# Summing experts' results by accumulating DMA in a graph and mixture-of-experts kernel

## The chip, the cores and the metric

The kernel runs on one core of a Trainium2 chip. The metric is the device time of one execution in microseconds (us), the median of several runs. The engines are named as in the profile: PE is TensorE (matrix products), PEld its weight loads, DVE is VectorE, ACT is ScalarE, POOL is GpSimd, SP is SyncE. SP, ACT and POOL issue DMAs; indirect DMAs (gathers and scatters by a list of rows) are issued by POOL.

## The reference

3125 nodes with 256 features each pass through four layers, each added to the nodes' rows: a graph convolution of three layers, a mixture of experts, a graph attention, and a second mixture of experts. The change is in the two mixtures. The first one has 16 experts:

```
gate_logits = x @ gate_w + gate_b
topk_vals, topk_idx = jax.lax.top_k(gate_logits, K)          # K = 2
topk_w = jax.nn.softmax(topk_vals, axis=-1)
h = jax.nn.relu(jnp.einsum('bsh,ehf->bsef', x, w1) + b1)
expert_out = jnp.einsum('bsef,efh->bseh', h, w2) + b2
sel = jnp.take_along_axis(expert_out, topk_idx[:, :, :, None], axis=2)
moe = jnp.sum(topk_w[..., None] * sel, axis=2)
y = x + moe                                                   # then a layer norm over y
```

The second has 8 experts, weights that are the softmax over all of them, GELU for ReLU, and adds the weighted sum to the nodes' rows without a norm; that is the kernel's output. In both, a node's result is its base row plus two experts' rows, each times a weight. The second bias b2 of an expert is part of its row.

## The kernel before

A tile is 128 nodes on 128 partitions; there are 25 node tiles (`NT`) of which 125 rows each are real. The expert stages don't work by node tile but by token tile: 128 tokens of one expert. A `Router` does this for each mixture.

`steps` computes the gate for some node tiles, chooses two experts a node, and scatters for each choice a record of eight numbers into `slots`, a list in HBM that is ordered by expert. `metas` holds the records: 0 is the place of the result, 1 the second expert, 2 and 3 the weights, 5 the node's number. `keep` writes the normalised rows into `feats` in HBM, from which they are gathered later. `steps` also fills `cw`, a table of nodes by experts with the weights. `plan` counts the tiles of each expert; `mine` has a 1 where token tile j belongs to expert e. `clear`, early in the kernel, fills the unused records and the unused result rows.

`experts` runs over token tiles: 58 in the first mixture, 54 in the second. For tile j, `fetch` loads its records (`slot`, L1021, by SP or ACT) and gathers its rows (`xs`, L1023, by POOL); `turned` transposes them (L1032, PE; L1034, DVE); `first` multiplies with w1, whose 512 KB SP loads per tile (L1009, L1044), and ACT applies the function (L1048); `second` multiplies with w2 into `py` (L1054). DVE then computes where the row goes and its weight g (L1061 to L1068), multiplies `py` by g into `y` (L1070), and POOL scatters y to rows of `res` in HBM (L1071). `res` has two rows a node, one per choice, and a row for each unused place, so every scattered row has a place of its own and the kernel declares the scatters independent of each other. The function `behind` keeps PE's and SP's instructions of this loop in the written order: products of tile j+1 with w1, transposes of tile j+2, products of tile j with w2. POOL's queue is filled by the scheduler, in which gathers run nine tiles ahead of the scatters.

The bias b2 is added by node tile, not by token tile: `cw` of a node tile is transposed and multiplied with b2 and added to the node's base row in SBUF. Eight node tiles are done before the loop (L1094 to L1107), the other 17 beside token tiles 8 to 24 (`bias`, L1081 to L1086).

After the loop, `results` loads the two result rows of each node (L1153, 256 KB a node tile), and PE adds them to the base row by three products with the identity (L1156), which ACT copies to SBUF (L1157). In the first mixture the layer norm, the transposes and products for the attention follow block by block (L1524 to L1549). In the second, each node tile goes to the output by two DMAs, from ACT and SP (L1745), 112 and 13 rows.

Of the kernel before, what the change touches and what calls it, by code (L numbers as in the profile page):

```python
# [19 lines left out]
P = 128  # L20
# [574 lines left out]
def fast(  # L595
# [136 lines left out]
    tok2 = consts.tile([P, NT], F32, name="tok2")  # L732
    nc.vector.tensor_scalar(tok2, iota_r[:, :NT], 2.0 * P, None, op0=OP.mult)
    nc.vector.scalar_tensor_tensor(tok2, part.to_broadcast([P, NT]), 2.0, tok2, op0=OP.mult, op1=OP.add)
# [6 lines left out]
    nc.vector.tensor_copy(metas[:, :, 0], tok2)  # L741
# [3 lines left out]
    class Router:  # L745

# [3 lines left out]
        def __init__(self, name, gate_w, gate_b, E, softmax, pool):  # L750
            self.name, self.E, self.softmax = name, E, softmax
            self.Q = E * NT + 3
            self.TT = -(-2 * N // P) + E
            self.slots = dram.tile([self.Q * P, 8], F32, name=f"slots_{name}")
            self.feats = dram.tile([NP, D], F32, name=f"feats_{name}")
            self.res = dram.tile([2 * NP + self.TT * P, D], F32, name=f"res_{name}")
            self.sent = []
            self.off = pool.tile([P, 2, NT], F32, name=f"off_{name}")
            for i in range(2):
                nc.vector.tensor_scalar(self.off[:, i, :], drop, float((E * NT + 1) * P + i * PADS), unreal,  # L760
                                        op0=OP.add, op1=OP.mult)
            self.gwt = pool.tile([P, DC, E], F32, name=f"gw_{name}")
            nc.sync.dma_start(self.gwt, gate_w.rearrange("(c p) e -> p c e", p=P))
            self.gbt = row_bcast(gate_b, E, f"gb_{name}", pool)
            self.cw = pool.tile([P, NT, E], F32, name=f"cw_{name}")

            self.seen = pool.tile([P, NT + 1, E], BF16, name=f"seen_{name}")
            nc.vector.memset(self.seen[:, 0, :], 0.0)
            self.at0 = pool.tile([P, E], F32, name=f"at0_{name}")
            nc.vector.tensor_scalar(self.at0, iota_r[:, :E], float(NP), None, op0=OP.mult)  # L770
            self.neg = pool.tile([P, E], F32, name=f"neg_{name}")
            nc.vector.tensor_scalar(self.neg, iota_r[:, :E], float(-E), None, op0=OP.add)

        def clear(self, room):

            Q = self.Q
            none = room[:NT, :2 * PADS * D]
            nc.gpsimd.memset(none, 0.0)
            nc.scalar.dma_start(self.res[:2 * NP, :].rearrange("(t p) d -> t (p d)", t=NT)[:, 2 * REAL * D:], none)
            b = room[:, :Q * 8].rearrange("p (q m) -> p q m", m=8)  # L780
            nc.gpsimd.memset(b, 0.0)
            at = room[:, Q * 8:Q * 9].bitcast(I32)
            nc.gpsimd.iota(at, pattern=[[1, Q]], base=0, channel_multiplier=Q)
            nc.vector.tensor_single_scalar(at, at, P - 1, op=OP.bitwise_and)
            nc.vector.tensor_scalar(b[:, :, 0], at, float(2 * NP), None, op0=OP.add)
            nc.gpsimd.memset(b[:, :, 1], -1.0)
            nc.gpsimd.memset(b[:, :, 4], 1.0)
            nc.scalar.dma_start(self.slots.rearrange("(p q) m -> p (q m)", p=P), room[:, :Q * 8])
# [6 lines left out]
        def keep(self, rows, t0, U):  # L795
            nc.gpsimd.dma_start(self.feats[t0 * P:(t0 + U) * P, :].rearrange("(u p) d -> p u d", p=P), rows)

        def steps(self, H, t0, U, work, psum, h0=None, pe=lambda i: i, kept=None):
# [68 lines left out]
            if not kept:  # L867
                self.keep(H[:, h0:h0 + U, :], t0, U)
# [12 lines left out]
            yield  # L881
            cw = self.cw[:, t0:t0 + U, :]
            w2 = wt("w2", [P, U, E])
            nc.vector.tensor_tensor(cw, hots[0], bc(meta[:, :, 2]), op=OP.mult)
            nc.vector.tensor_tensor(w2, hots[1], bc(meta[:, :, 3]), op=OP.mult)
            nc.vector.tensor_tensor(cw, cw, w2, op=OP.add)
# [38 lines left out]
        def plan(self, pool, psum):  # L925
# [26 lines left out]
            nc.tensor.matmul(pe[:, 1, :], ones_f[:E + 1, :], place, start=True, stop=True)  # L952
            self.ebc = pool.tile([P, TT], F32, name="ebc")
# [20 lines left out]
        def experts(self, w1, w2all, func, base, pool, psum, psy, beside=None):  # L974

# [5 lines left out]
            self.done = []  # L981
            AHEAD = 6
            EARLY = 8
# [67 lines left out]
            def second(j, r, slot, hid):  # L1051
                py = psy([P, D], "py")
                for c in range(FC):
                    behind(nc.tensor.matmul(py, hid[:, c, :],  # L1054
                                            w2all[:, bass.ds(r, 1), c, :].rearrange("p o d -> p (o d)"),
                                            start=(c == 0), stop=(c == FC - 1)), "PE")

                m = [slot[:, i:i + 1] for i in range(5)]
# [3 lines left out]
                to = pool.tile([P, 1], F32, name="to", bufs=16)  # L1062
                nc.vector.scalar_tensor_tensor(to, m[4], float(P * j), m[0], op0=OP.mult, op1=OP.add)
                to_i = pool.tile([P, 1], I32, name="to_i", bufs=16)
                nc.vector.tensor_tensor(to_i, to, two, op=OP.add)
# [5 lines left out]
                d = nc.gpsimd.indirect_dma_start(  # L1071
                    out=self.res, out_offset=bass.IndirectOffsetOnAxis(ap=to_i, axis=0), in_=y, in_offset=None)
                for o in self.done:
                    tc.declare_no_dep(d.ins, o.ins, reason="every row has a place of its own")
                self.done.append(d)
                if EARLY <= j < NT:
                    bias(j)

            def bias(j):
                pc = psum([E, P])  # L1080
                nc.tensor.transpose(pc, self.cw[:, j, :], ident)  # L1081
                cT = pool.tile([E, P], F32, name="cT", bufs=3)
                nc.scalar.copy(cT, pc)
                pi = psum([P, D])
                nc.tensor.matmul(pi, cT, b2t, start=True, stop=True)
                nc.vector.tensor_tensor(base[:, j, :D], base[:, j, :D], pi, op=OP.add)  # L1086


            cTs = {}

            def by_expert(j0):
                pc = psum([E, 4, P])
                for i in range(4):
                    nc.tensor.transpose(pc[:, i, :], self.cw[:, j0 + i, :], ident)  # L1094
                cTs[j0] = pool.tile([E, 4, P], F32, name="cT4", bufs=2)
                nc.scalar.copy(cTs[j0], pc)

            by_expert(0)
            for j0 in range(0, EARLY, 4):
                if j0 + 4 < EARLY:  # L1100
                    by_expert(j0 + 4)
                for i in range(0, 4, 2):
                    pi = psum([P, 2, D])
                    for k in range(2):
                        nc.tensor.matmul(pi[:, k, :], cTs[j0][:, i + k, :], b2t, start=True, stop=True)
                    to = base[:, j0 + i:j0 + i + 2, :D]
                    nc.vector.tensor_tensor(to, to, pi, op=OP.add)  # L1107
# [41 lines left out]

        def results(self, base, t, pool, psum):  # L1150

            r = pool.tile([P, 2, D], F32, name="r", bufs=10)
            nc.sync.dma_start(r, self.res[2 * P * t:2 * P * (t + 1), :].rearrange("(p k) d -> p k d", k=2))  # L1153
            p = psum([P, D])
            for k, v in enumerate((r[:, 0, :], r[:, 1, :], base[:, t, :])):
                nc.tensor.matmul(p, ident, v, start=(k == 0), stop=(k == 2))  # L1156
            nc.scalar.copy(base[:, t, :], p)  # L1157
# [18 lines left out]
    with tc.tile_pool(name="edges", bufs=1) as ed, tc.tile_pool(name="ework", bufs=2) as ew:  # L1176
# [134 lines left out]
        with tc.tile_pool(name="ps_cnt0", bufs=2, space=PSUM) as ps_cnt0, \  # L1311
# [6 lines left out]
            for b, (s0, bw) in enumerate(BLK):  # L1318
                cr = ew.tile([P, NT, bw], F16, name="cr", tag="cr")
                nc.gpsimd.memset(cr.rearrange("p t (u q) -> p t u q", q=P)[:, :, :, REAL:], 0.0)  # L1320
                for dt in range(s0 // P, (s0 + bw) // P):
# [31 lines left out]
                    if dt == 1:  # L1353
                        R0.clear(HB[:, 9 * R1.Q:])
                        R1.clear(HB[:, :9 * R1.Q])
# [131 lines left out]
    with tc.tile_pool(name="moe0", bufs=1) as mp:  # L1487
        with tc.tile_pool(name="ps_moe0", bufs=2, space=PSUM) as ps:
# [13 lines left out]
            with tc.tile_pool(name="w2all", bufs=1) as wp:  # L1502
                R0.experts(f0_w1, R0.second_weights(f0_w2, wp), AF.Relu, HBn, mp, misc0, big0, add_beta)
        with tc.tile_pool(name="ps_pre", bufs=2, space=PSUM) as ps, tc.tile_pool(name="tail", bufs=1) as mp:
            def rsum(shape):
                return ps.tile(shape, F32, name="rsum", tag="rsum")

# [9 lines left out]
            for s0, w in BLK:  # L1517
                t0, n = s0 // P, w // P
                for t in range(t0, t0 + n):
                    R0.results(HBn, t, mp, rsum)  # L1520
# [59 lines left out]
    with tc.tile_pool(name="gat", bufs=2) as gp, tc.tile_pool(name="aloads", bufs=2) as loads:  # L1580
        xp = gp.tile([P, NT, NH, OD], F32, name="xp", bufs=1)
        with tc.tile_pool(name="ps_att", bufs=2, space=PSUM) as ps_att, \
# [34 lines left out]
            def finish(b, att, sums):  # L1617
# [64 lines left out]
                R1.keep(hh[:, :ns_, :], t0, ns_)  # L1682
# [50 lines left out]
    with tc.tile_pool(name="moe1", bufs=1) as mp, tc.tile_pool(name="ps_moe1", bufs=2, space=PSUM) as ps:  # L1733
# [6 lines left out]
        R1.experts(f1_w1, w2one, AF.Gelu, X, mp, misc1, big1)  # L1740
        with tc.tile_pool(name="tail", bufs=1) as mp:
            for t in range(NT):
                R1.results(X, t, mp, misc1)
                for q, a, b in ((nc.scalar, 0, SPLIT), (nc.sync, SPLIT, REAL)):
                    q.dma_start(out[REAL * t + a:REAL * t + b, :], X[a:b, t, :])  # L1745
# [36 lines left out]
```

## Time and profile before

| what | value |
|---|---|
| median of three runs | 2034.19 us (2029.81 to 2035.13) |
| the profiled execution, its own time | 2044.37 us |
| its span, first to last instruction | 2042.6 us |
| mean granted PE clock in it | 0.959 |
| PE busy | 1872.3 us (92%) |
| DVE busy | 1184.0 us (58%) |
| ACT busy | 788.7 us (39%) |
| POOL busy | 366.8 us (18%) |

A profile row of an operation gives the line of the kernel, the engine, the operation, what it writes and reads, how often, its busy time, and the idle time of its engine just before it with what ended that (the releaser). A timeline row gives start, duration, and in brackets the idle time before with its releaser. The chain of waits is followed back from the last instruction: at each step to what released it. The page cuts the span into 40 slices of 51 us, and gives for each the busy share in tenths:

```profile
PE   1898979999999999699998979999999998799997
DVE  7998863113103545544432958988898998444420
POOL 4000000000000132344451000000300402444530
DMA  6145663344344434765675401111111111455746
```

The graph convolution takes the slices up to about the sixteenth, the first mixture those to the twenty-second, the attention those to the thirty-fourth, and the second mixture the last six. The two mixtures are where POOL has 4s and 5s.

### The profile page before, as it was taken

The page shows a single profiled execution, that of the slowest core. Times are in us where ns is not written, and L with a number is a line of the kernel's source. Part 1 is how long each engine was busy: PE and PEld are TensorE (multiplying, and loading weights), DVE is VectorE, ACT ScalarE, POOL GpSimd, SP SyncE. Part 2 cuts the span into 40 slices and gives each one's busy share as a digit, 9 for nine tenths or more (in the row PEclk, how much of TensorE's full clock was granted, in tenths as well). Part 3 has the DMA queues.
Part 4 walks back from the last instruction along what each step waited for, and adds up shares of the span by engine and source line. Part 5 has one row for each costly group of instructions (what it writes and reads, how often), then busy time and mean ns, then how long its engine had stood idle before and what let it go on. Part 6 is the DMA issues. An engine that isn't in the chain of part 4 may idle for free.

```text
span 2042.6 us, 31794 instructions
## 1 busy us (share of the span) xinstructions
PE 1872.3 (92%) x10844; PEld 1238.8 (61%) x10844; DVE 1184.0 (58%) x3785; ACT 788.7 (39%) x1600; POOL 366.8 (18%) x414
## 2 busy tenths in 40 slices
PE   1898979999999999699998979999999998799997
PEld 1444548898898779588897622222223233688995
DVE  7998863113103545544432958988898998444420
ACT  0367766556557555123322660212212222232321
POOL 4000000000000132344451000000300402444530
PEclk9999989999999999699998969999999999699998
DMA  6145663344344434765675401111111111455746
GB/s 165 41 176 221 230 230 118 118 117 138 120 116 145 125 104 119 234 200 166 197 215 159 147 13 52 50 40 50 41 43 50 39 40 29 127 188 171 207 153 199
DMA packets 172299, 259.90 MB, mean 127 GB/s; under 512 B 33476, under 2 KB 116658, under 8 KB 171100
## 3 DMA queue, kind: packets, MB, share of 16 engines
q1 hardware_dynamic: 148446, 211.87, 33.8%
q0 software_dynamic: 16016, 37.00, 5.5%
q10 hardware_dynamic: 7662, 8.84, 1.4%
q8 instruction: 92, 1.51, 0.3%
q14 instruction: 83, 0.68, 0.1%
HBM read 187.38 MB, written 70.27 MB: 126 GB/s over the span
## 4 chain that ended last, share of the span: by engine, by line
PE 58%; issue 12%; DVE 12%; POOL 9%; ACT 5%; DMA 4%; SPq 0%; POOLq 0%; ACTq 0%; another core or an unknown queue 0%; DVEq 0%
PE agg L1437 20%; PE att L1598 12%; PE sums L1598 7%; POOL res_m L1071 5%; POOL xs L1023 4%; PE gout L1446 3%; DVE od L1332 3%; PE pc L1334 2%; PE misc L1156 2%; DMA res_m<-y,to_i 2%; PE pt L1343 2%; DVE HB L1710 1%; PE ph L1044 1%; PE pl L1598 1%; PE misc L823 1%
## 5 line engine op out<-in xcount | busy, mean ns | idle before, releaser
L1437 PE MATMUL agg<-ar,parts 128*128 128x512 f32 (+1 forms) x2100 | 446.6, 371 | 7.6 <-DMA cload<-cnt 7.6
L1437 PEld LDWEIGHTS agg<-ar,parts 128*128 128x128 f32 x2100 | 382.3, 189 | 55.0 <-ACT parts L1425 7.7
L1710 DVE SCALAR_TENSOR_TENSOR HB<-ub,wj,cload 128x512 f32<-128x512 f32 (+1 forms) x420 | 268.3, 684 | 22.3 <-ACT ub L1614 9.2
L1432 ACT CAST ar<-cload 128x2560 fp32r<-128x2560 f16 (+1 forms) x105 | 220.7, 2102 | 143.5 <-PE agg L1437 130.2
L1048 ACT ACTIVATE hid<-ph,b1s 128x128 f32<-128x128 f32 x448 | 127.7, 368 | 306.3 <-issue 154.4
L1044 PEld LDWEIGHTS ph<-xsT,w1t 128*128 128x128 f32 x1792 | 222.9, 197 | 27.5 <-issue 13.5
L1044 PE MATMUL ph<-xsT,w1t 128*128 128x128 f32 x1792 | 235.4, 283 | 3.8 <-DVE xsT L1034 2.7
L1054 PE MATMUL py<-w2all,hid 128*128 x896 | 211.9, 380 | 0.0
L1598 PE MATMUL att<-HB,xp 128*64 128x512 f32 (+1 forms) x840 | 186.7, 563 | 0.0
L1440 DVE COPY aT<-agg 128x512 f32<-128x512 f32 (+1 forms) x21 | 13.3, 634 | 277.6 <-PE agg L1437 277.6
L1054 PEld LDWEIGHTS py<-w2all,hid 128*128 128x128 f32 x896 | 162.1, 191 | 17.5
L1332 DVE TENSOR_SCALAR od<-ramp,by 128x450 f16<-128x450 f16 (+11 forms) x588 | 151.4, 316 | 21.5 <-PE pc L1334 20.3
L1334 PE MATMUL pc<-od,os 128*128 128x450 f16 (+11 forms) x588 | 136.3, 332 | 18.6 <-DVE od L1332 10.5
L911 POOL DMA_INDIRECT slots_m<-metas,places x100 | 105.3, 1053 | 204.3 <-DVE places L909 110.0
L1071 POOL DMA_INDIRECT res_m<-y,to_i x112 | 110.4, 985 | 167.8 <-DVE y L1070 156.5
L1023 POOL DMA_INDIRECT xs<-feats_m,slot x112 | 108.2, 966 | 104.4 <-PE misc L1032 56.9
L1034 DVE COPY xsT<-misc 128x256 f32<-128x256 f32 x112 | 47.4, 423 | 134.6 <-PE misc L1032 66.0
L1598 PEld LDWEIGHTS att<-HB,xp 128*64 128x64 f32 x840 | 51.9, 136 | 107.0 <-issue 61.3
L1337 ACT CAST cr<-pc 128x400 f16<-128x400 f32 (+10 forms) x202 | 95.5, 503 | 51.0 <-PE pc L1334 49.4
L1334 PEld LDWEIGHTS <-os 128*128 128x128 f16 x588 | 62.0, 117 | 78.9 <-DVE od L1332 21.9
L1598 PE MATMUL sums<-HB,pj 128*32 128x512 f32 (+1 forms) x840 | 102.2, 558 | 0.0
L1070 DVE TENSOR_SCALAR y<-py,g 128x256 f32<-128x256 f32 x112 | 54.1, 483 | 81.4 <-PE py L1054 80.6
(333 smaller groups left out, 2300.0 us busy)
## 6 DMA issues: line engine op xcount, KB each, us to landing
cload<-cnt SPq DMA_DIRECT2D x60, 640.0 KB
w1t<-in_L_ffn_w_dram SPq DMA_DIRECT2D x56, 512.0 KB
w1t<-in_L_ffn_W_dram SPq DMA_DIRECT2D x52, 512.0 KB
cload<-cnt SPq DMA_DIRECT2D x45, 480.0 KB
cntT<-ct SPq DMA_DIRECT2D x100, 128.0 KB
cnt<-cr SPq DMA_DIRECT2D x4, 3200.0 KB
cload<-cntT SPq DMA_DIRECT2D x20, 640.0 KB
r<-res_m SPq DMA_DIRECT2D x50, 256.0 KB
```

The lines of the kernel that those rows point to most:

```text
L911: d = nc.gpsimd.indirect_dma_start(out=self.slots, out_offset=bass.IndirectOffsetOnAxis(ap=at_i[:, u:u + 1], axis=0), in_=meta[:, u, :], i ...
L1023: nc.gpsimd.indirect_dma_start(out=xs, out_offset=None, in_=self.feats, in_offset=bass.IndirectOffsetOnAxis(ap=slot[:, 5:6].bitcast(I32), ...
L1044: behind(nc.tensor.matmul(ph[:, c, :], w1t[:, f, c * P:(c + 1) * P], xsT[:, f, :], start=(f == 0), stop=(f == DC - 1)), "PE")
L1048: nc.scalar.activation(hid[:, c, :], ph[:, c, :], func, bias=self.b1s[:, c, j:j + 1])
L1054: behind(nc.tensor.matmul(py, hid[:, c, :], w2all[:, bass.ds(r, 1), c, :].rearrange("p o d -> p (o d)"), start=(c == 0), stop=(c == FC - 1 ...
L1071: d = nc.gpsimd.indirect_dma_start(out=self.res, out_offset=bass.IndirectOffsetOnAxis(ap=to_i, axis=0), in_=y, in_offset=None)
L1332: nc.vector.tensor_scalar(od[:, :w * NT], ramp[:, :w * NT], by[1][:, j:j + 1], None, op0=OP.is_equal)
L1334: nc.tensor.matmul(pc[:, :w * NT], os_[:, :, j % OS], od[:, :w * NT], start=(k == 0), stop=(k == c - 1))
L1432: nc.scalar.copy(ar[:, :, :w], a[:, :, :w])
L1437: nc.tensor.matmul(agg[f][:, :w], parts[:, t, i, f * P:(f + 1) * P], ar[:, k, :w], start=(t == 0 and i == 0), stop=(t == NT - 1 and i == 1))
L1598: return chain(nc.tensor.matmul(*args, **kw))
L1710: nc.vector.scalar_tensor_tensor(e[:, h, :w], ub[:, h, :w], wj[:, t, h:h + 1], a[:, k, :w], op0=OP.max, op1=OP.mult)
```

## The change

The results of the experts are no longer written to rows of their own and summed afterwards. `sums` in HBM has one row a node. `keep` now writes the base rows into it too (the normalised rows in the first mixture, the nodes' rows in the second), and every token tile's scatter adds to it (`compute_op=OP.add`). Since a node's two rows come from two tiles, the scatters of a mixture are no longer declared independent: each waits for the one before it. A record's first number is now the node's number as an integer, which the scatter reads straight from the slot tile; unused records point to 128 rows behind the nodes'.

```
-            self.res = dram.tile([2 * NP + self.TT * P, D], F32, name=f"res_{name}")
+            self.sums = dram.tile([NP + P, D], F32, name=f"sums_{name}")
...
-        def keep(self, rows, t0, U):
-            nc.gpsimd.dma_start(self.feats[t0 * P:(t0 + U) * P, :].rearrange("(u p) d -> p u d", p=P), rows)
+        def keep(self, rows, base, t0, U):
+            for to, v in ((self.feats, rows), (self.sums, base)):
+                nc.gpsimd.dma_start(to[t0 * P:(t0 + U) * P, :].rearrange("(u p) d -> p u d", p=P), v)
```

The bias b2 becomes part of each token tile's product: a product of the tile's column of `mine`, repeated to 128 columns, with b2 opens the sum in `py`. `cw`, its three DVE operations in `steps`, `bias` and the early bias work go away, and two DVE operations per token tile that computed the place:

```
             def second(j, r, slot, hid):
                 py = psy([P, D], "py")
+                behind(nc.tensor.matmul(py, self.mine[:E, j:j + 1].to_broadcast([E, P]), b2t, start=True, stop=False),
+                       "PE")
                 for c in range(FC):
                     behind(nc.tensor.matmul(py, hid[:, c, :],
                                             w2all[:, bass.ds(r, 1), c, :].rearrange("p o d -> p (o d)"),
-                                            start=(c == 0), stop=(c == FC - 1)), "PE")
+                                            start=False, stop=(c == FC - 1)), "PE")
...
-                d = nc.gpsimd.indirect_dma_start(
-                    out=self.res, out_offset=bass.IndirectOffsetOnAxis(ap=to_i, axis=0), in_=y, in_offset=None)
-                for o in self.done:
-                    tc.declare_no_dep(d.ins, o.ins, reason="every row has a place of its own")
-                self.done.append(d)
-                if EARLY <= j < NT:
-                    bias(j)
+                nc.gpsimd.indirect_dma_start(
+                    out=self.sums, out_offset=bass.IndirectOffsetOnAxis(ap=slot[:, 0:1].bitcast(I32), axis=0),
+                    in_=y, in_offset=None, compute_op=OP.add)
```

`results` goes away. After the first mixture, SP loads the finished rows, two node tiles at a time, 14 loads in all; after the second, they are copied from `sums` to the output, five node tiles at a time, from HBM to HBM:

```
-                for t in range(t0, t0 + n):
-                    R0.results(HBn, t, mp, rsum)
+                for t in range(t0, t0 + n, 2):
+                    m = min(2, t0 + n - t)
+                    nc.sync.dma_start(HBn[:, t:t + m, :],
+                                      R0.sums[t * P:(t + m) * P, :].rearrange("(u p) d -> p u d", p=P))
...
-        with tc.tile_pool(name="tail", bufs=1) as mp:
-            for t in range(NT):
-                R1.results(X, t, mp, misc1)
-                for q, a, b in ((nc.scalar, 0, SPLIT), (nc.sync, SPLIT, REAL)):
-                    q.dma_start(out[REAL * t + a:REAL * t + b, :], X[a:b, t, :])
+        to = out.rearrange("(t p) d -> p t d", p=REAL)
+        of = R1.sums[:NP, :].rearrange("(t p) d -> p t d", p=P)
+        for t in range(0, NT, 5):
+            for q, a, b in ((nc.scalar, 0, SPLIT), (nc.sync, SPLIT, REAL)):
+                q.dma_start(to[a:b, t:t + 5, :], of[a:b, t:t + 5, :])
```

## The prediction

> **What bounds the kernel now.** I read the page's chain of waits by engine and line, then the busy time by stretch for the two expert stages, then POOL's timeline inside and at the end of them, then the chain in order of time around their two ends. Busy time first (columns: busy us of PE, PE weight loads, DVE, ACT, POOL; granted clock; DMA share; GB/s):
>
> ```profile
> 875.00:1100.00 225.00, 224.18 (x1493) 201.52 (x1492) 87.83 (x367) 68.16 (x241) 101.13 (x104) 1.00 0.60 185
> 1777.00:1990.00 213.00, 212.04 (x1409) 190.23 (x1408) 83.49 (x346) 64.11 (x227) 94.78 (x97) 1.00 0.60 183
> ```
>
> PE is busy in all of both stretches, at full clock, and POOL in under half. Both stages are PE's. POOL's timeline shows what a tile takes:
>
> ```profile
> 951.45 0.99 POOL L1071 DMA_INDIRECT res_m<-y,to_i  x1 [1.29 <-DVE y L1070]
> 953.87 0.97 POOL L1023 DMA_INDIRECT xs<-feats_m,slot  x1 [1.44 <-PE misc L1032]
> 956.13 0.99 POOL L1071 DMA_INDIRECT res_m<-y,to_i  x1 [1.29 <-DVE y L1070]
> ...
> 1041.40 0.99 POOL L1071 DMA_INDIRECT res_m<-y,to_i  x1 [1.29 <-DVE y L1070]
> 1042.88 0.97 POOL L1023 DMA_INDIRECT xs<-feats_m,slot  x1 [0.49 <-issue]
> 1045.13 0.99 POOL L1071 DMA_INDIRECT res_m<-y,to_i  x1 [1.28 <-DVE y L1070]
> ```
>
> A tile takes 956.13−951.45 = 4.68 us where `bias` runs beside it, and 1045.13−1041.40 = 3.73 us elsewhere. Every scatter (L1071) waits for its y, never for the scatter before it. The one place where a scatter does wait for a landing is the end of the second stage:
>
> ```profile
> 1990.91 0.97 POOL L1071 DMA_INDIRECT res_m<-y,to_i  x1 [2.54 <-DVE y L1070]
> 1993.59 0.97 POOL L1071 DMA_INDIRECT res_m<-y,to_i  x1 [1.71 <-DMA res_m<-y,to_i]
> ```
>
> So one step of plain scatters in a chain is 1993.59−1990.91 = 2.68 us. The chain in order of time gives the landing times, and the tail that the change removes:
>
> ```profile
> 1756.10 4.05 DMA slots_m<-metas,places
> 1760.18 1.55 DMA slot<-slots_m
> 1761.80 0.76 issue
> 1762.56 3.62 DMA xs<-feats_m,slot
> ...
> 1993.59 2.60 DMA res_m<-y,to_i
> ...
> 1996.65 2.54 DMA r<-res_m
> 1999.19 34.29 PE misc L1156 x144
> ```
>
> A scatter of 128 rows into HBM takes 2.60 us from issue to landing, a gather of 128 such rows out of HBM 3.62. After the last landing PE sums three operands per node tile for 34.29 us.
>
> **PE's share of the change.** Removed: 17 `bias` calls a stage (tiles 8 to 24), 4.68−3.73 = 0.95 us each, 16.2 us a stage. Added: one product of b2 with `mine` per tile, two PE instructions over 256 columns like those of py. Six such instructions start 1.30 us apart in the tail (2030.28 to 2031.58), so two take 0.43 us; the old bias product on 16 rows (L1085, mean 426 ns, overlapping) is of that kind. 58 tiles in the first stage and 54 in the second: 24.9 and 23.2 us. PE's balance: +8.7 and +7.0, together **+15.7 us**; a tile becomes 3.73+0.43 = 4.16 us on PE. The product comes before its tile's hidden rows are needed, so it adds no wait.
>
> **The early bias work** (L1094 to L1107, about 9 us of PE at half clock, from 847.63 to 856.7) lies under the wait for slots and the first gather, which PE gets at 861.5: its removal gains nothing. If it kept PE's clock awake, its loss costs up to 5 us; I take 0.
>
> **The chain.** All scatters of a stage now add into `sums`, so each waits at the head of POOL's queue until the one before it has landed. Queued behind it are gathers; nine are issued before the first scatter, so each has many tiles of time and PE doesn't wait for them while the chain keeps pace. A slot tile (10 buffers) is now held until its scatter has landed, and SP's next slot load waits for that, with weight loads behind it: this only ties PE to the chain, and costs nothing beyond the chain's own rate. What decides is one step T of the chain against PE's 4.16 us.
>
> No row shows an accumulating scatter. Bounds on T:
> - below: the plain step, 2.68 us;
> - above: a gather and a scatter one after the other, 3.62+2.60+0.08 (the wait's own end, 2.68−2.60) = 6.30 us.
>
> Between: the plain step, 2.68; the read of the old row out of HBM, 3.62−2.60 = 1.02; a third descriptor per row, if POOL's 0.99 us writes two, 0.49. That is 4.19. The gather of 3.62 us was timed where DMA was lightly used (75 GB/s from 1740 to 1765), while the stages move 185 GB/s; the 4.05 us of a slots scatter against 2.60 shows that a landing can stretch by 1.45. I add 0.4, my choice, and take **T = 4.6 us**. It is nearer the lower bound since read and write share one issue and one completion.
>
> Here a rule says otherwise. The Trainium skill's page "DMA: Bandwidth & Descriptors", section "Anatomy of one DMA — SWDGE (gpsimd) path", has about 2.0 us of fixed cost plus bytes at 436 GB/s. For 128 KB that is 2.3 us, where the trace has 2.60; doubled reading makes it 2.6, and a chain step with 0.08 is 2.7. By the rule PE stays the bound and the change gains; by the rows, with an HBM read that costs 1.02 us more whatever its bytes, the chain is the bound. I go by the rows. Against the change speaks "Collectives: The Full Stack", section "The bandwidth ceiling: the fold count and why AG ≠ RS ≠ AR": an add in the DMA path needs two source reads on one ring and runs at about half a copy's rate. The trace of before has no such add, so it neither agrees nor differs.
>
> **The chain's sum.** Scatters now start from 874.40 to 1102.86 (57 steps) and from 1779.20 to 1993.59 (53 steps): 228.5+214.4 = 442.9 us. With T = 4.6, 110 steps are 506.0: **+63.1 us**. The last landing of each stage comes 4.3 instead of 2.6 us after its issue: +3.4.
>
> **The tails.** Second: from the landing at 1996.19 to the end at 2042.6 is 46.4 us. After: ten transfers from `sums` to `out`, 3.2 MB. The old tail moved 266 to 292 GB/s in its busy stretches; at 280 that is 11.4 us, plus 0.4 for the issue and the 7.4 us that follow the last product's copy (issue at 2035.28 to the end): 19.2. **−27 us**; if HBM to HBM runs at half that rate, −16. First: `results` took PE until 1120.5 before DVE got its first block; now 14 loads of half the bytes feed DVE about 8 us earlier, at 1112. DVE is the next bound (54.9 of 86 us from 1104 to 1190, gaps of 2 us after 1122), and the last block's ACT and PE steps stay. **−8 us**, between −15 and +3.
>
> **Routing and clearing.** Three DVE operations (0.22 us each at the costliest) leave every call of `steps`; about 0.4 us of each stage's start lay on the chain, and some in the DVE-bound attention. −2 us. `keep` issues a second transfer (0.8 us on POOL, seven times a layer), and 3.2 MB more are written in each layer; POOL has 6 to 12 us free between a keep and the slots that follow, and DMA's share there is 0.1 to 0.4: nothing. Without that cover it would be 0.8 us a block. `clear`: alike in size, nothing.
>
> **Sum.** +63.1+3.4−27−8−2 = +29.5 us: 2073.9 from the profiled execution's 2044.4. That one ran 10 us above the median of 2034.2; the same difference from the median gives **2064 us**. In general the change is 110·T−476.5; zero is at T = 4.33. A measurement of this kernel tells 0.3% (6 us) from no change: faster below T = 4.28, slower above 4.39.
>
> **The rivals.**
> - *Chain bound near my T* (4.39 to 5.2; +6 to +96, 2040 to 2130): 0.44, the forecast.
> - *PE stays the bound* (T up to 4.28). For it: the rule above, and a plain step of 2.68 with 1.5 us to spare. Against: the gather's 3.62. Time: 15.7−27−8−2+3 = −18 us, **2016**: 0.31. If scatters weren't ordered at all it would be the same time; the changed program's waits say that they are, each on its predecessor's semaphore.
> - *Chain and PE level*, within 0.3%: 0.06.
> - *The landing is far dearer* (T above 5.2, up to 6.3): +217 at the upper bound, **2251**: 0.19. For it: the read, add and write of 128 rows serialised under 185 GB/s of weights. Against: rows of a scatter go out side by side, and landings of 2.60 leave little time per row.
>
> Faster 0.31, same 0.06, slower 0.63. The range, 2006 to 2185 us, takes in PE-bound with better tails, and T up to 5.7 (+150); the likeliest case alone has 2040 to 2130.
>
> **What would show it.** In the changed profile scatters should start every 4.6 us in both stages with POOL idle before each until the DMA of `sums`, and PE at about 0.9 busy. The tail should end some 19 us after the last landing, with no PE work in it. If the scatters wait for y at 4.16 us a tile, the chain is cheap and I am wrong in sign; if PE falls below 0.8 busy, my read cost is too small.

## The result and the profile after

The changed kernel takes 2235.22 us (median of four runs, 2228.1 to 2241.53) against 2032.0 us before, a ratio of 1.099 (95% interval 1.097 to 1.101): slower by 203 us. The direction is the forecast's, the size more than six times its +30. The profiled execution took 2228.1 us with a span of 2226.1; its mean granted PE clock is 0.935 (before 0.959).

The scatters cut the execution into stages. From the timelines of both kernels:

| stretch | before, us | after, us | change |
|---|---|---|---|
| start to the first scatter | 874.4 | 868.7 | −5.7 |
| first to last scatter, first mixture (58 tiles) | 228.5 | 342.1 | +113.6 |
| to the first scatter of the second mixture | 676.3 | 684.6 | +8.3 |
| first to last scatter, second mixture (54 tiles) | 214.4 | 311.5 | +97.1 |
| last scatter to the end | 49.0 | 19.1 | −29.9 |
| sum | 2042.6 | 2226.0 | +183.4 |

The sum is the difference of the two profiled executions; the medians lie 20 us further apart. The stretches between the scatters lost 210.7 us, more than the whole. The busy time by stretch for the two stages (columns as before: busy us of PE, weight loads, DVE, ACT, POOL; clock; DMA share; GB/s):

```profile
870.00:1210.00 340.00, 278.08 (x1559) 222.10 (x1559) 73.19 (x260) 64.91 (x225) 138.33 (x106) 0.95 0.53 124
1897.00:2205.00 308.00, 258.84 (x1445) 208.94 (x1444) 66.49 (x235) 58.62 (x206) 126.78 (x97) 0.94 0.54 126
```

PE, busy without a gap before, now rests 18% of the time in the first stage and 16% in the second, and DMA moves 124 GB/s in place of 185. No engine and no queue is full, so what rules is a chain of waits. The rows of the page that have it (in such a row the two figures between the bars are busy us and mean ns, and behind them stands the idle time before):

```profile
L1052 DVE TENSOR_SCALAR two<-slot,ebc 128x1 f32<-128x1 f32 x112 | 23.8, 213 | 431.3 <-DMA slot<-slots_m 431.3
L1058 POOL DMA_INDIRECT sums_m<-y,slot x112 | 177.6, 1586 | 255.9 <-DMA sums_m<-y,slot 178.2
```

The scatter's waits for the scatter before (178.2 us) were forecast. The first row was not: DVE stood 431.3 us before `two`, an operation on 128 numbers, until a slot tile was loaded. Most of the stage repeats in rounds of four tiles. POOL's timeline has four scatters of one, which start 9.33, 4.64 and 5.50 us after one another:

```profile
982.64 1.58 POOL L1058 DMA_INDIRECT sums_m<-y,slot  x1 [2.69 <-DMA sums_m<-y,slot]
984.70 1.01 POOL L1012 DMA_INDIRECT xs<-feats_m,slot  x1 [0.48 <-PE py L1045]
990.68 0.98 POOL L1012 DMA_INDIRECT xs<-feats_m,slot  x1 [4.97 <-DMA slot<-slots_m]
991.97 1.62 POOL L1058 DMA_INDIRECT sums_m<-y,slot  x1 [0.30 <-DVE y L1057]
996.61 1.58 POOL L1058 DMA_INDIRECT sums_m<-y,slot  x1 [3.02 <-DMA sums_m<-y,slot]
998.50 1.02 POOL L1012 DMA_INDIRECT xs<-feats_m,slot  x1 [0.31 <-issue]
1002.11 1.58 POOL L1058 DMA_INDIRECT sums_m<-y,slot  x1 [2.60 <-DMA sums_m<-y,slot]
```

SP's issues and DVE in the same time:

```profile
982.69 0.38 SPq L998 DMA_DIRECT2D w1t<-in_L_ffn_w_dram  x1
987.68 0.34 SPq L1010 DMA_DIRECT2D slot<-slots_m  x1
...
996.04 0.34 SPq L1010 DMA_DIRECT2D slot<-slots_m  x1
996.63 0.38 SPq L998 DMA_DIRECT2D w1t<-in_L_ffn_w_dram  x1
```

```profile
989.90 0.21 DVE L1052 TENSOR_SCALAR two<-slot,ebc 128x1 f32<-128x1 f32 x1 [5.00 <-DMA slot<-slots_m]
990.03 0.27 DVE L1054 TENSOR_SCALAR g<-slot,ebc 128x1 f32<-128x1 f32 x1
990.21 0.47 DVE L1057 TENSOR_SCALAR y<-py,g 128x256 f32<-128x256 f32 x1
```

Follow the stall. The scatter of 982.64 lands at 987.5, 4.85 us after its issue (completion events of the trace). That frees a slot buffer, and SP issues its next slot load at 987.68. It ends DVE's wait at 989.90, and only then comes the y that the next scatter takes.

Which slot DVE waits for is told by its order in the trace: counted from the first tile on, `two` of tile j+9 stands ahead of y of tile j in one of four tiles, in the others that of tile j+8. With ten slot buffers, slot j+9 lies where slot j−1 was. The scatter reads its row numbers from the slot tile, so that one is now held until scatter j−1 has landed. So y of tile j, and with it scatter j, waits for a landing and then a slot load. In the kernel before, `two` even stands ten tiles ahead, but there the scatter reads a tile of its own (`to_i`), and a slot is free once DVE and the gather have read it. POOL's gathers have the same pattern: in the tiles with the stall a gather that needs slot j+9 stands ahead of scatter j (990.68 in the timeline), and holds POOL for 1.3 us after y is there.

The second thing to see is in the 5.50 us step without a stall: SP issues a tile's w1t (512 KB) 0.02 us after the scatter's start, at 996.63, since it stands behind a slot load that the landing let go (996.04). That scatter lands after 4.77 us; the one before it, of 991.97, has its w1t 4.7 us behind it and lands after 3.88. The tile view of `sums` in the first stage gives the landings:

```profile
DMA to landing us min/median/max: 3.8/4.7/6.0
```

### The profile page after: what moved, and what is told of

It is laid out like the page before. It is cut to its first block, busy times and chain, and to the rows that moved or that the text cites. A ratio compares the mean times of both kernels' runs of the same rounds, so it can differ in the third digit from the quotient of the medians.

```text
span 2226.1 us, 30800 instructions
## 1 busy us (share of the span) xinstructions
PE 1894.1 (85%) x10618; PEld 1205.8 (54%) x10618; DVE 1138.2 (51%) x3484; ACT 761.4 (34%) x1512; POOL 445.3 (20%) x426
## 5 line engine op out<-in xcount | busy, mean ns | idle before, releaser
L1033 PE MATMUL ph<-xsT,w1t 128*128 128x128 f32 x1792 | 248.6, 297 | 95.7 <-DVE xsT L1023 95.7
L1033 PEld LDWEIGHTS ph<-xsT,w1t 128*128 128x128 f32 x1792 | 233.3, 208 | 127.7 <-DVE xsT L1023 125.5
L1052 DVE TENSOR_SCALAR two<-slot,ebc 128x1 f32<-128x1 f32 x112 | 23.8, 213 | 431.3 <-DMA slot<-slots_m 431.3
L1058 POOL DMA_INDIRECT sums_m<-y,slot x112 | 177.6, 1586 | 255.9 <-DMA sums_m<-y,slot 178.2
L1045 PE MATMUL py<-w2all,hid 128*128 x896 | 226.9, 397 | 0.0
L1541 PE MATMUL att<-HB,xp 128*64 128x512 f32 (+1 forms) x840 | 191.4, 578 | 0.0
L793 POOL DMA_DIRECT2D feats_m<-HB x7 | 5.6, 798 | 459.8 <-DVE HB L703 450.6
```

The costliest lines, as they stand in the source:

```text
L1033: behind(nc.tensor.matmul(ph[:, c, :], w1t[:, f, c * P:(c + 1) * P], xsT[:, f, :], start=(f == 0), stop=(f == DC - 1)), "PE")
L1045: behind(nc.tensor.matmul(py, hid[:, c, :], w2all[:, bass.ds(r, 1), c, :].rearrange("p o d -> p (o d)"), start=False, stop=(c == FC - 1)), ...
L1058: nc.gpsimd.indirect_dma_start(out=self.sums, out_offset=bass.IndirectOffsetOnAxis(ap=slot[:, 0:1].bitcast(I32), axis=0), in_=y, in_offset ...
L1541: return chain(nc.tensor.matmul(*args, **kw))
```

## The experiments

Ratios are to the kernel before, run beside on the same chip (its median was 2032 to 2049 us on the several chips); "stages" are first to last scatter of the two mixtures in the profiled execution.

**Sixteen slot buffers.**

```
-                slot = pool.tile([P, 8], F32, name="slot", bufs=AHEAD + 4)
+                slot = pool.tile([P, 8], F32, name="slot", bufs=AHEAD + 10)
```

> The changed kernel with 16 slot buffers in place of 10. Theory (each fourth tile stalls because the second gather of a pair waits at POOL for a slot tile that can be loaded only when the scatter just issued has landed; this is what turned steps of 5.5 us into 6.1 a tile): the 5 us waits of xs for the slot's DMA disappear, and the stages fall from 6.1 to about 5.5 us a tile: about 60 to 80 us less, 2155 to 2175 us. The chain itself stays: scatters still wait for the landing of the one before, 5.5 us apart. Rival A (the four-tile stall comes from the order of gathers and scatters on POOL or from the loads' own latency, not from the buffer): within 10 us of the changed kernel's 2235. Rival B (the buffer is all that lifts the step over my forecast of 4.6): about 2065.

Ratio 1.035 (1.031 to 1.039); stages 276.7 and 253.8 us, 123 us less than with ten. The direction is the theory's, the size above it: most steps of 5.5 us went as well, the median step is now 4.63. POOL's timeline in mid-stage, then SP's w1t loads:

```profile
1006.74 1.60 POOL L1058 DMA_INDIRECT sums_m<-y,slot  x1 [1.83 <-DMA sums_m<-y,slot]
1008.64 0.99 POOL L1012 DMA_INDIRECT xs<-feats_m,slot  x1 [0.30 <-issue]
1011.40 1.59 POOL L1058 DMA_INDIRECT sums_m<-y,slot  x1 [1.76 <-DVE g L1055]
```

```profile
1004.98 0.38 SPq L998 DMA_DIRECT2D w1t<-in_L_ffn_w_dram  x1
1009.53 0.38 SPq L998 DMA_DIRECT2D w1t<-in_L_ffn_w_dram  x1
1014.08 0.38 SPq L998 DMA_DIRECT2D w1t<-in_L_ffn_w_dram  x1
```

The loads now come every 4.55 us and mostly between scatters (here 2.8 us after one). That rhythm is PE's, as the bias product below shows. A scatter lands in 3.86 us (median, from the completion events) and the next starts 0.77 us after it. Since 4.63 is a little more than 4.55, the loads drift towards the scatter, and at times one meets it:

```profile
981.43 1.59 POOL L1058 DMA_INDIRECT sums_m<-y,slot  x1 [2.31 <-DVE y L1057]
987.60 1.59 POOL L1058 DMA_INDIRECT sums_m<-y,slot  x1 [3.28 <-DMA sums_m<-y,slot]
```

```profile
982.23 0.38 SPq L998 DMA_DIRECT2D w1t<-in_L_ffn_w_dram  x1
```

Here w1t comes 0.8 us after the scatter, which lands after 5.40 us. The six scatters of this run with a load 0.8 to 1.1 us behind them land after 5.3 to 5.7 us, later than with the load at the very start (4.8).

**The plain scatters chained.**

```
-                for o in self.done:
-                    tc.declare_no_dep(d.ins, o.ins, reason="every row has a place of its own")
-                self.done.append(d)
```

> The kernel before, with its plain scatters chained: only the declarations that scatters are independent are gone, so each scatter waits for the landing of the one before, but nothing is added up in DRAM. Theory (the accumulating write is what makes a step long): a plain step of 2.7 to 3.4 us stays under PE's 3.73 us, PE stays the bound, 2025 to 2045 us. Rival (the wait for a landing is dear whatever is written, by the wake-up of POOL and by the load of the stage): steps of 4.5 us and more, 2120 or above.

Ratio 1.006 (1.004 to 1.008); stages 229.8 and 227.3 us. The first stage keeps its time within 1.4 us, the second loses 13 us in single steps of 5 to 6 us. At the first stage's end, in POOL's timeline, the chain alone sets the step:

```profile
1091.98 0.97 POOL L1071 DMA_INDIRECT res_m<-y,to_i  x1 [2.19 <-DMA res_m<-y,to_i]
1095.13 0.97 POOL L1071 DMA_INDIRECT res_m<-y,to_i  x1 [2.18 <-issue]
1098.29 0.97 POOL L1071 DMA_INDIRECT res_m<-y,to_i  x1 [2.18 <-DMA res_m<-y,to_i]
```

3.15 to 3.16 us a step: about 2.41 to land and 0.75 until POOL starts. Accumulating steps in the same place of the other runs take 4.5. So an accumulating step costs about 1.35 us more; POOL's own time for it is 0.59 longer (1.58 against 0.99). The two scatters also differ in the tile that holds the row numbers; the gather reads them from the slot tile too, and POOL needs only about 1.0 for it.

**Four sums in turn**, with sixteen slot buffers.

```
-                    out=self.sums, ...
+                    out=self.parts[j % 4], ...
```

> The changed kernel with 16 slot buffers and four sums tensors, taken in turn by the tiles, so that a scatter waits only for the landing of the fourth one before it; each is still an accumulating scatter of the same size. Base is written to all four, and only the first is copied to the output and on to the next layer, so the output leaves out three quarters of the experts' rows. Theory (waiting for the landing is the price, not the added-up transfer): scatters wait for y, a tile takes PE's 4.16 us, stages of about 240 and 225 us, about 2035 to 2050 us (six more block writes of base among it). Rival (the accumulating transfer itself is the limit, its traffic or the POOL time of 1.6 us for its descriptors): tiles of 5 us or more, above 2120.

Ratio 1.018 (1.015 to 1.022); stages 258.3 and 238.9 us, a step of 4.55 us with hardly a deviation, every mid-stage scatter waiting for y. The theory's cause holds: accumulating scatters that needn't wait for the one before are no limit. Its tile time, 4.16, was wrong.

**The bias product alone**, in the kernel before (the changed `second` without its scatter; no `bias`, no `cw`).

> The kernel before with only the biases changed: one product of b2 per token tile beside the tile's own products, no bias work by node tile and no table of weights by expert. Theory (my balance of PE's work): 24.9+23.2 us added and 32.4 us taken away, +15.7 us, less about 2 for routing: about 2046 us, ratio 1.007. Rival A (the product's weights and wait for py's buffer cost more than 0.43 us, as 0.6 us a tile): about 2065. Rival B (it hides, and the removal of early work shows): 2015 to 2030.

Ratio 1.034 (1.030 to 1.037), near rival A's size: stages 257.3 and 239.1 us, PE busy throughout, 4.55 us a tile. The price was 0.82 us, not 0.43.

**The same with 128 rows.**

Changed against the run before this one:

```
-            self.b2t = pool.tile([self.E, D], F32, name="b2t")
+            self.b2t = pool.tile([P, D], F32, name="b2t")
+            nc.gpsimd.memset(self.b2t, 0.0)
...
-  self.mine[:E, j:j + 1].to_broadcast([E, P])
+  self.mine[:, j:j + 1].to_broadcast([P, P])
```

> The run with the bias product, with its operands padded by zero rows from 16 to 128 rows, so that the product has the shape of py's own products. Theory A (what lifts the product from 0.43 to 0.82 us a tile is its 16-row shape: the weight loads around it don't run beside products): tiles of about 4.16 us, the stages 236 and 220 us, 42 us less than with 16 rows, ratio to before about 1.013. Theory B (any weight load of a broadcast column, or any group more, costs this): 4.55 us a tile as before, ratio 1.034.

Theory A held: ratio 1.0105 (1.008 to 1.013), 4.16 us a tile, stages 235.2 and 218.9 us. PE's timeline, first with 16 rows, then with 128 (each row covers instructions of one kind, xcount):

```profile
999.79 0.38 PE L1027 MATMUL misc<-ident,xs 128*128 128x128 f32 x2
1000.10 0.69 PE L1048 MATMUL py<-b2t,mine 16*128 16x256 f32 x2
1000.72 1.99 PE L1051 MATMUL py<-w2all,hid 128*128 x8
1002.55 1.95 PE L1039 MATMUL ph<-xsT,w1t 128*128 128x128 f32 x16
```

```profile
1003.13 0.38 PE L1030 MATMUL misc<-ident,xs 128*128 128x128 f32 x2
1003.35 0.60 PE L1051 MATMUL py<-b2t,mine 128*128 128x256 f32 x2
1003.78 1.89 PE L1054 MATMUL py<-w2all,hid 128*128 x8
1005.51 0.72 PE L1042 MATMUL ph<-xsT,w1t 128*128 128x128 f32 x5
```

From start to start the 16-row product takes 0.62 us, the 128-row one 0.43; the py products after it 1.83 and 1.73, and the transposes ahead 0.31 and 0.22. Eight times the rows, 0.39 us less. In the second mixture the narrow product has 8 rows and costs the same: 4.55 us a tile there too. Why PE loses this time around a product of few rows isn't shown.

**The bias on DVE**, first in the kernel before, then in the changed kernel with sixteen slots.

```
+                b2s[j] = pool.tile([P, D], F32, name="b2row", bufs=5)
+                behind(dma.dma_start(b2s[j], self.b2[bass.ds(e, 1), :].to_broadcast([P, D])), name)
...
+                nc.vector.tensor_tensor(yb, py, b2s.pop(j), op=OP.add)
```

> The kernel before with only the biases changed, and without PE: the b2 row of the tile's expert is loaded over all partitions beside the tile's w1t, and DVE adds it to py before scaling. Theory (the stages are PE's, at 3.73 us a tile when no bias work stands beside it): 17 x 0.95 us go in each stage, about 2 in routing: 34 us less, ratio 0.983. Rival (128 KB more per tile delay w1t or DVE's y delays py's buffer): no gain or a loss, ratio 1.00 to 1.02.

The rival: ratio 1.009 (1.007 to 1.011). Some steps keep PE's 3.7 us, but every few tiles one takes 5 to 6: DVE waits 70 us for slots between 930 and 1090 us, and scatters land after about 5.4 us in place of 2.4 (as far as their completion events were recorded). DMA is busy for 0.80 of that time.

> The changed kernel with both of its other prices taken off: 16 slot buffers, and the bias added on DVE from a loaded row, so that a tile takes PE 3.73 us. What is left is one chain of accumulating scatters. Theory (an undisturbed step is a landing of 3.85 us and 0.75 us to POOL's next start, 4.6 us): stages of about 262 and 244 us, no better than 8 to 25 us below the run with 16 slots alone; ratio to before about 1.02 to 1.03. Rival A (in the run with 16 slots PE set the pace and the chain could go faster): steps of 4.2 us or less, ratio 1.00. Rival B (PE no longer keeps the loads of w1t at a fixed distance from the scatters, so more of them meet, landings of 4.8 us): steps of 5 us and more, ratio 1.04 or above.

Ratio 1.117 (1.113 to 1.120): rival B, well above its figures, and slower than the changed kernel although PE has less to do. Steps of 6.8 us, landings of 6.0; b2 row and w1t are both issued within 0.6 us of the scatter's start. But two things differ here, PE's pace and 128 KB more per tile. The next pair separates them.

**Sixteen slots and the 128-row product** (both changes as above), then the same **without w1t loads** (this change alone is shown).

```
-                w1t = first_w1.pop(j) if j in first_w1 else weights(j, e, nc.sync, "SP")
+                w1t = first_w1[j % FIRST]
```

> The changed kernel with 16 slot buffers and the bias product padded to 128 rows: PE's tile is 4.16 us, below a chain step of 4.6. Theory (a chain that is the bound pulls the loads of w1t into its own rhythm: each is issued as a scatter starts, and that landing takes 4.7 in place of 3.85 us): steps of about 5.5 us, though PE has less to do than with 16 slots alone: stages of some 300 and 285 us, ratio to before 1.06 to 1.07. Rival (in the run with the bias on DVE it was the loads of b2 rows that slowed the chain; without them it keeps 4.6 us): stages of 262 and 244 us, ratio about 1.02 to 1.03.

> The run before this one, without the loads of w1t: only the first two tiles' weights are loaded, and all tiles take them in turn, so the output leaves out the other experts' first weights. Theory (the loads of w1t are what stretches landings): every landing takes 3.8 us and every step 4.5 to 4.6 us in the whole stage, stages of about 260 and 242 us, ratio to before about 1.02. Rival (another neighbour of the scatter, as the gather or the slot load, stretches it): landings of 4.5 us and more in mid-stage as in the run before this one.

The first: ratio 1.059 (1.057 to 1.061), stages 304.4 and 280.4 us: 54 us more than with sixteen slots alone, for 0.39 us **less** PE work a tile. From mid-stage on, SP's w1t starts with each scatter, behind a slot load that the landing let go:

```profile
1004.85 0.34 SPq L1013 DMA_DIRECT2D slot<-slots_m  x1
1005.44 0.38 SPq L1001 DMA_DIRECT2D w1t<-in_L_ffn_w_dram  x1
```

```profile
1005.43 1.59 POOL L1061 DMA_INDIRECT sums_m<-y,slot  x1 [2.72 <-DMA sums_m<-y,slot]
```

The second run: 1.060 (1.058 to 1.062), the time of the run before, as its rival would have it, but not the rival's landings. Tile views of `sums` in the first stage, with and without the loads:

```profile
DMA to landing us min/median/max: 3.6/4.7/6.3
```

```profile
DMA to landing us min/median/max: 3.7/3.8/5.4
```

Without the loads nine of ten landings take at most 3.94 us, and three of four steps about 4.5 to 4.65. It is w1t that stretches them. (Other weights route other nodes: the second mixture has 57 tiles here, so its stage can't be compared.) The first stage has 294.8 us, only 9.6 less, because every fourth step takes 6.4 to 8.3 us: in this kernel's DVE order `two` stands fifteen tiles ahead of y, and with sixteen buffers that is again the slot of the scatter just issued.

**w1t issued by ACT**, ten slots kept (the number of the tile's expert is read on ACT then, too).

```
-                w1t = first_w1.pop(j) if j in first_w1 else weights(j, e, nc.sync, "SP")
+                w1t = first_w1.pop(j) if j in first_w1 else weights(j, e, nc.scalar, "ACT")
```

> The changed kernel, 10 slot buffers kept, with the w1t loads issued by ACT in place of SP, so that they no longer stand behind a slot load that waits for a landing. Theory (steps of 5.5 us where no slot is waited for are a landing of 4.8 in place of 3.85 us, because SP issues 512 KB of w1t at the very moment of the scatter): three of four steps fall to about 4.6 us while the stall of each fourth tile stays: some 2.7 us less per four tiles, 70 us in all, ratio to before about 1.065. Rival A (landings are slower for the slot load or another cause): ratio stays at 1.10. Rival B (the stall of the fourth tile also came from w1t in front of the slot load): ratio 1.035 as with 16 slots.

Ratio 1.096 (1.093 to 1.099): no gain, as rival A had it, though not for its reason. Landings did fall to 3.86 us (median) and many steps to 4.5 to 4.7, but others took 5 to 6 or 8 to 9 with waits for y. DVE's waits for slots remain: 121.9 us between 930 and 1130, in the changed kernel 148.9. So shorter landings alone gain nothing while the slots hold the tiles up; which wait made the other steps longer wasn't followed.

**PE kept busy in the first tail.**

```
+                for t in range(t0, t0 + n):
+                    warm = ps.tile([P, D], F32, name="warm", tag="warm")
+                    for k in range(3):
+                        nc.tensor.matmul(warm, ident, HBn[:, t, :], start=(k == 0), stop=(k == 2))
```

> The changed kernel with three products by the identity for each node tile put back into the first tail (150 PE instructions; their sum is read by nobody), after each tile's load from sums. Theory A (the first tail gained 1 in place of my 8 us because PE, with no products left to sum, runs at half clock there): the granted clock in the tail rises from 0.5-0.67 to 0.9 and more, and the stretch from the last scatter of the first stage to the first attention product falls from 92.7 us to 86-88. Rival B (that stretch is DVE's, whatever PE's clock): clock up, stretch within 1.5 us of 92.7. Rival C (the products hold up PE's own work): stretch longer by 2 to 5 us.

Theory A held: from the last scatter (1215.31) to the first attention product (1300.73) 85.4 us in place of 92.7. Ratio 1.092 (1.087 to 1.097), which doesn't tell 7 us from nothing; the stretch does: in the five other runs that differ from the changed kernel in their stages alone it is 92.4 to 93.6 (one execution each). Busy time by stretch (the clock is the number before the DMA share), first the changed kernel, then with the added products:

```profile
1236.00:1256.00 20.00, 15.21 (x44) 6.14 (x44) 15.14 (x73) 9.30 (x25) 0.00 (x0) 0.67 0.32 122
1256.00:1276.00 20.00, 14.54 (x42) 5.69 (x40) 14.63 (x76) 8.77 (x25) 0.00 (x0) 0.67 0.00 1
```

```profile
1240.00:1260.00 20.00, 20.00 (x94) 13.28 (x93) 15.41 (x76) 10.15 (x29) 0.00 (x0) 1.00 0.33 128
1260.00:1280.00 20.00, 19.42 (x94) 12.91 (x92) 18.59 (x93) 11.87 (x34) 0.00 (x0) 1.00 0.00 1
```

**The kernel before with 128-row bias products**, its bias still by node tile (`b2t` padded as above, and the transposed table held in three zeroed tiles of 128 rows).

```
-                cT = pool.tile([E, P], F32, name="cT", bufs=3)
-                nc.scalar.copy(cT, pc)
+                cT = wide[j % 3]
+                nc.scalar.copy(cT[:E, :], pc)
```

> The kernel before, its bias work by node tile kept, with b2 padded by zero rows to 128 and the transposed table of weights held in zeroed tiles of 128 rows, so that each bias product has 128 rows in place of 16. Theory (a 16-row product costs 0.39 us more of PE than a 128-row one, as the two runs with the bias product show): 17 calls a stage at 0.95-0.39 = 0.56 us, 13 us less in all, ratio 0.9935. Rival (the call's 0.95 us is its transposition, or the gap is that product's alone where weights are a broadcast column): ratio 0.999 to 1.001.

Ratio 0.9972 (0.9962 to 0.9981), between theory and rival. A tile with a `bias` call beside it takes 4.49 us in place of 4.68, so a call costs 0.76 in place of 0.95: a gain of 0.19, half of the 0.39 that was expected. The call still transposes into 16 rows, which may be the rest; that wasn't tried. It is the only version here that is faster than the kernel before, by 0.3%.

## Why the prediction missed

- **"Costs nothing beyond the chain's own rate"**, said of the slot tile that is held until its scatter has landed, is the step that failed. It was put at nothing and cost 65.4+57.7 = 123 us (ten buffers against sixteen). I had seen the hold and SP's wait, but counted ten buffers against the distance of the scatters, and did not look at what stands ahead of y in DVE's order and ahead of the scatter in POOL's. Both had an instruction that needs the slot of tile j+9. In a round of four tiles, 24.7 us, against 4×4.63 = 18.5: the stall has 9.0−4.63 = 4.4 us of the excess (0.9 of it a stretched landing), the two other stretched steps 2×0.87 = 1.7. With the stall gone the chain is what the prediction had in mind: with sixteen buffers the two stages are 530.5 us, forecast 506.0; most of the 24.5 us between lies in twenty single steps above 5 us.
- **The step T.** My 4.6 us is what an undisturbed step takes (4.5 at the ends of stages, 4.63 with sixteen buffers), but that is luck, by two errors against each other: I had a landing of 4.5 under load (and 4.3 where I summed the last landings) and 0.08 until the next start; measured are 3.86 and 0.77. The 0.08 came from the last scatter, which I took for a link of a chain. Its step of 2.68 us is shorter than any of the chained plain run, where the shortest is 3.15. Of my 0.4 for a loaded stage at most 0.13 is due to the load as such; what counts is whether a load of w1t starts with the scatter, and then it is 0.9, or about 1 us behind it, and then it is 1.4 to 1.9. My test "PE below 0.8 busy shows the read cost too small" didn't speak (PE was 0.82 and 0.84 busy), and would have blamed the wrong term.
- **The two rules on T.** The estimate from the Trainium skill's "DMA: Bandwidth & Descriptors" (section "Anatomy of one DMA — SWDGE (gpsimd) path"), fixed cost plus bytes, gave 2.7 us for an accumulating step; measured are 4.5, and 3.15 for a plain one. Rows were the better guide. The half rate of an add in "Collectives: The Full Stack" (section "The bandwidth ceiling: the fold count and why AG ≠ RS ≠ AR"), a figure for large transfers around a ring, fits the direction; how much of the 1.35 us here is bytes, no run tells.
- **PE's balance** of +15.7 us was +53.5 (257.3−228.5 and 239.1−214.4). The failed term is 0.43 us a tile, taken from products on 128 rows; with 16 it is 0.82. I had taken the old 16-row product for one of that kind by its mean duration, 426 ns. But the matmuls overlap, and durations don't tell the cost: 426 is also the mean where the product costs 0.82. The starts in the trace of before do tell it, 0.63 us for two:

```profile
951.15 0.69 PE L1085 MATMUL misc<-b2t,cT 16*128 16x256 f32 x2
951.78 1.60 PE L1044 MATMUL ph<-xsT,w1t 128*128 128x128 f32 x12
```

In the changed kernel this hid behind the chain; with the stall gone it is level with it, at 4.55 against 4.63. From here the stages' +210.7 can be read as 53.5 for PE, 34.1 for the chain above it (sixteen slots against the bias product alone), 123.1 for the slots. The rival "PE stays the bound, 2016 us" could not have come true: without a chain it is, by my estimate from these figures, about 2032+53.5−30 = 2056, and the run with four sums, where no scatter waits for the one before it, has ratio 1.018.
- **Tails.** The second gained 29.9 us, forecast 27 less 1.7 for the later landing: right within 5 us. The first was to gain 8 and gained 1. DVE did get its first rows early, 8.4 us after the last scatter in place of 12.2, but PE, which lost 150 products there, was granted half its clock for much of the tail, and that took the gain away: with the products added back the tail is 7.3 us shorter.
- **Routing and early bias**: −5.7 us to the first scatter, forecast some −2 for both; one execution each doesn't bear this out, since versions that leave this part alone have 867 and 872 us where the kernel before has 874. What lies between the mixtures besides the tail lengthened by 9 us, where I had forecast a small gain. From the first to the last attention product it is 541.5 us at a granted clock of 0.97, before 530.3 at 0.98. The bias product alone, in the kernel before, has 540.2 at 0.97, the plain chain on the same chip 533.9 at 0.98. So it seems to come with the change of the biases; why the clock drops there wasn't tried.

## What to carry to other kernels

A wait added at the end of a loop lengthens the life of every buffer that the waiting instruction reads: count buffers against the furthest instruction ahead of the critical one in each engine's real order, not against the distance in the source. (A copy of the row numbers in a tile of its own, as before, would be the other remedy; it wasn't tried.) When a chain of DMAs becomes the bound, it sets the rhythm of everything that waits for it, so loads start together with the chain's next link and slow it; a PE tile only a little shorter than the chain's step (4.55 against 4.63 us here) made shorter stages than one well below it (4.16). And price a product by the starts of instructions around one of its own shape, not by its duration.

## What the runs showed of the hardware

- A product on 16 rows (two instructions, between products on 128) takes PE 0.39 us more than the same with zeros up to 128 rows, by the starts in the two timelines: 0.19 at the product, 0.10 in the products after it, 0.09 in the transposes before.
- POOL takes 1.58 us to issue an accumulating scatter of 128 rows, 0.99 a plain one; it lands after 3.8 us, a plain one after 2.4, both in a quiet stretch. From a landing to the start of a scatter that waited for it POOL needs 0.75 us.
- The same accumulating scatter lands after 4.8 us when a 512 KB load is issued with it, after 5.3 to 5.7 when the load comes 0.8 to 1.1 us later (six scatters with sixteen slots), and after 3.9 (median) when it comes 1.5 us later or more. With 128 KB more beside it, and the load 0.5 us behind the scatter, it takes 6.0.
- PE without enough work in the first tail was granted 0.50 to 0.67 of its clock; with 150 idle products it had 0.79, then 1.00, then 0.67, and the work came out 7 us earlier.
